# Order of the neighbour products in a residual block: one PSUM bank after the other, or both in turn

## Chip, core and metric

The kernel runs on one core of a Trainium2 chip. The metric is device time in microseconds (us) from the start to the end of one execution, lower is better; a figure for a kernel is the median of several executions.

## What is computed

The program is a chain of four layers on a batch of 4 sequences of 256 tokens with 512 features. The first two layers (a mixture of low-rank updates, and a cross-attention with 32 heads and a layer norm) give `x`. The last two are the same function, applied one after the other, and this is where the change lies:

```
idx = _knn_indices(xyz, 8)            # 8 nearest of 512 points, the same in both layers
for i in range(4):
    shortcut = points                  # [4, 256, 512]: 256 channels, 512 points
    p = _lrelu(points)
    g = _group_point(p, idx_t)         # the 8 neighbours of each point
    c  = einsum('oi,bin->bon',   w_center[i],   p)
    gn = einsum('oi,bikn->bokn', w_neighbor[i], g)
    points = (c + gn.sum(axis=2)) / 9 + shortcut
```

`w_center` and `w_neighbor` are the same array here (256 x 256 for each `i`). So a block is `points += W (p (I + N)) / 9`, where `N` is the 512 x 512 matrix of zeros and ones that says which points are neighbours of which. Two layers of four blocks make 8 blocks in a row for each of the 4 sequences.

## The kernel before

**Tiling.** `x1[b]` holds one sequence as two tiles of 128 channels x 512 points (`NL` = 2, the index `o` or `l`). `nbr[b, m]`, m = 0 to 3, holds the 128 rows 128m to 128m+127 of `I + N` as a 128 x 512 tile in fp32r (one pass of TensorE). `fT` holds the transposed weights.

**One block, `block(b, i)`.**
1. VectorE makes `p`, the leaky ReLU of both tiles of `x1[b]` (line 857).
2. TensorE makes `(W p)` transposed, in two halves of 256 points, `m2` = 0 and 1 (line 869): one PSUM bank `wp` holds two groups of 128 points x 256 output channels. Each half is 4 fp32 products, which the trace shows as 8 matmuls.
3. The half is split in two fp32r tiles, so that two one-pass products together keep fp32's accuracy: ScalarE casts it to `hi` (`wph`, line 882), VectorE subtracts `hi` from the PSUM bank to get `lo` (`wpl`, line 885).
4. The neighbour products (line 900, the function `gather`): for each output tile `o` a PSUM bank `pb[o]` (named `blk`) takes the sum over the four `m` and over `hi` and `lo` of `part.T @ nbr[b, m]`: 8 matmuls of 128 x 128 weights and 512 moving columns for each `o`, half of them from `m2` = 0 and half from `m2` = 1. `hi` and `lo` are the weights that are loaded, `nbr` is what streams.
5. VectorE adds a ninth of each bank to `x1[b]` (line 912). After the last block each tile goes out by a DMA of the SP queue (line 922).

**Order.** Nothing runs in the order of the source. `plan.add` records each step with an engine, an estimated cost, and what it reads and writes (the short forms `pe`, `act`, `dve`, `pool`); `Plan.emit` then plays a list scheduler: at each turn it takes, of the steps that could start first, the one of lowest rank (a due time from `DEADLINES` less the length of the chain behind it), and issues its instructions. One `pe(...)` is one unit that other PE work cannot be placed into. A PSUM bank is taken from the 8 by the first step that names it and given back after the last. So the four sequences run interleaved: while the half tile of one is split, PE works for another. Because `gather` is added once for each (`m2`, `o`), each such step is 4 matmuls into one bank, and `pb[0]` and `pb[1]` are separate outputs of separate steps.

Of the kernel before, what the change touches and what calls it, by code (L numbers as in the profile page):

```python
# [24 lines left out]
NL = S // 128  # L25
# [139 lines left out]
def xattn_seq_kernel(ctx: ExitStack, tc: tile.TileContext, a: dict, out: bass.AP):  # L165
# [23 lines left out]
    def make(kind, place, name):  # L189
# [4 lines left out]
    pe, act, dve, pool = (  # L194
        lambda *args, _e=e, **kw: plan.add(_e, *args, **kw) for e in ("PE", "ACT", "DVE", "POOL")
    )
# [11 lines left out]
    nbr = {}  # L208
# [642 lines left out]
    def block(b, i):  # L851
        pt, wi = x1[b], fT[:, i % NBLK]
        p = Buf("full", f"p{b}_{i}")
        for l in range(NL):
            dve(
                0.69,
                lambda l=l: V_.scalar_tensor_tensor(p.tile[:, l], pt[:, l], SLOPE, pt[:, l], ALU.mult, ALU.max),  # L857
                (("x", b, l), p),
                (("p", b, l),),
                port=True,  # L860
            )
        parts = []
        for m2 in range(2):
            ps = Buf("bank", f"wp{b}_{i}_{m2}")
            hi, lo = Buf("wp", f"wph{b}_{i}_{m2}"), Buf("wp", f"wpl{b}_{i}_{m2}")
            pe(
                1.73,
                lambda ps=ps, m2=m2: [
                    T_.matmul(  # L869
                        ps.tile[:, bass.ts(k, S)],  # L870
                        lhsT=p.tile[:, c, bass.ts(2 * m2 + k, 128)],
                        rhs=wi[:, c, :],
                        start=(c == 0),
                        stop=(c == NL - 1),
                    )
                    for k in range(2)
                    for c in range(NL)
                ],
                (("p", b, 0), ("p", b, 1), p, "fT"),
                (ps, hi, lo),  # L880
            )
            act(0.59, lambda ps=ps, hi=hi: A_.copy(hi.tile, ps.tile), (ps,), (hi,))  # L882
            dve(
                0.69,
                lambda ps=ps, hi=hi, lo=lo: V_.tensor_tensor(  # L885
                    lo.tile, ps.tile, hi.tile.bitcast(F32), ALU.subtract
                ),
                (ps, hi),
                (lo,),
            )  # L890
            parts.append((hi, lo))
        pb = [Buf("bank", f"blk{b}_{i}_{o}") for o in range(NL)]

        for m2 in range(2):
            for o in range(NL):

                def gather(m2=m2, o=o):
                    for m in (2 * m2, 2 * m2 + 1):
                        for k, part in enumerate(parts[m2]):
                            T_.matmul(  # L900
                                pb[o].tile,
                                lhsT=part.tile[:, bass.ds(m % 2 * S + o * 128, 128)],
                                rhs=nbr[b, m],
                                start=(m == 0 and k == 0),
                                stop=(m == H // 128 - 1 and k == 1),
                            )

                pe(0.92, gather, (*parts[m2], ("nbr", b, 2 * m2), ("nbr", b, 2 * m2 + 1)), (pb[o],))
        for o in range(NL):
            dve(  # L910
                0.69,
                lambda o=o: V_.scalar_tensor_tensor(  # L912
                    pt[:, o], pb[o].tile, 1.0 / (KNN + 1.0), pt[:, o], ALU.mult, ALU.add
                ),
                (pb[o],),
                (("x", b, o),),
            )
            if i == 2 * NBLK - 1:
                plan.add(
                    "SP",  # L920
                    0.45,
                    lambda o=o: S_.dma_start(out=out[b, bass.ts(o, 128), :], in_=pt[:, o, :]),
                    (("x", b, o),),
                )
# [4 lines left out]
    for b in range(B):  # L929
        plan.batch = b  # L930
        if b == B - 1:
            load_xT(b)
            load_x(b)
        mixture(b)
        values(b)
        queries(b)
        nearest(b)
        for i in range(2 * NBLK):
            plan.unit = (b, i)
            block(b, i)  # L940
        plan.unit = None
# [50 lines left out]
```

## Time and profile before

| | |
|---|---|
| time, median of 3 runs (lowest to highest) | 406.25 us (405.9 to 406.34) |
| the profiled execution's own time | 406.27 us |
| its span, first to last instruction | 404.5 us |
| granted TensorE clock, mean | 0.998 |
| PE busy | 398.3 us (98%), 2324 matmuls |
| VectorE busy | 264.7 us (65%) |
| ScalarE busy | 130.4 us (32%) |
| GpSimd busy | 93.0 us (23%) |
| neighbour products (line 900) | 512 matmuls |
| `wp` products (line 869) | 512 matmuls |

The span is what the trace covers; 1.8 us lie around it. The busy times are of one execution. The ends of matmul rows are modelled, so that a row's own length (0.39 to 0.58 us for line 900) is longer than the step from one start to the next; the steps between starts are what the work costs.

### The profile page before, as it was taken

How to read it: one execution, taken by the hardware profiler on the slowest of the kernel's cores; microseconds unless marked ns; L12 is line 12 of the kernel's file. 1: busy time of each engine (PE TensorE's matmuls, PEld its weight loads, DVE VectorE, ACT ScalarE, POOL GpSimd, SP SyncE). 2: the span in 40 equal slices, each digit the busy share in tenths (PEclk: the TensorE clock that was granted, in tenths of full speed). 3: DMA queues.
4: the chain of work that ended last, by engine and by line, in shares of the span. 5: the costliest groups of instructions: out<-in, count | busy, mean ns of one | idle time of the engine just before them, and what ended most of it. 6: DMA issues, size and time to landing. Idle time of an engine off the chain costs nothing.

```text
span 404.5 us, 5757 instructions
## 1 busy us (share of the span) xinstructions
PE 398.3 (98%) x2324; PEld 306.6 (76%) x2324; DVE 264.7 (65%) x476; ACT 130.4 (32%) x234; POOL 93.0 (23%) x94
## 2 busy tenths in 40 slices
PE   8999999999999999999999999999999999999996
PEld 6755786656857767866778888888888888888884
DVE  3855659997999999745588644646455463635433
ACT  4652153555464485131244222111111111111110
POOL 4644320727945808605000000000000000000000
PEclk9999999999999999999999999999999999999999
DMA  6995100000000000000000000000000000010102
GB/s 229 364 421 210 52 2 0 2 2 0 2 2 0 2 2 1 2 2 0 0 0 2 0 2 0 0 2 0 2 0 1 2 0 0 2 52 1 53 0 104
DMA packets 4746, 15.33 MB, mean 38 GB/s; under 512 B 688, under 2 KB 816, under 8 KB 4080
## 3 DMA queue, kind: packets, MB, share of 16 engines
q1 hardware_dynamic: 4720, 14.97, 9.9%
q8 instruction: 18, 0.29, 0.3%
q14 instruction: 8, 0.07, 0.1%
HBM read 12.87 MB, written 2.10 MB: 37 GB/s over the span
## 4 chain that ended last, share of the span: by engine, by line
PE 98%; DVE 1%; ACT 0%; issue 0%
PE blk L900 29%; PE wp L869 27%; PE upd L448 7%; PE o L818 7%; PE q L670 7%; PE pT L786 3%; PE d L512 3%; PE avT L798 2%; PE v L632 2%; PE route L392 2%; PE s L711 2%; PE kT L578 2%; PE d L525 1%; PE zT L438 1%; PE nbrT L556 1%; PE x1T L477 1%
## 5 line engine op out<-in xcount | busy, mean ns | idle before, releaser
L869 PE MATMUL wp<-fT,p 128*128 128x256 f32 x512 | 119.0, 380 | 0.0
L900 PE MATMUL blk<-nbr,wph 128*128 128x512 f32 x256 | 109.8, 429 | 0.0
L869 PEld LDWEIGHTS wp<-fT,p 128*128 128x128 f32 x512 | 96.6, 189 | 16.8 <-issue 1.2
L900 PE MATMUL blk<-nbr,wpl 128*128 128x512 f32 x256 | 100.6, 393 | 0.9 <-DVE wpl L885 0.9
L912 DVE SCALAR_TENSOR_TENSOR x<-blk,x 128x512 f32<-128x512 f32 x64 | 43.8, 687 | 76.9 <-PE blk L900 76.9
L882 ACT CAST wph<-wp 128x512 fp32r<-128x512 f32 x64 | 37.6, 587 | 168.4 <-PE wp L869 168.4
L885 DVE TENSOR_TENSOR wpl<-wp,wph 128x512 fp32r<-128x512 f32 x64 | 44.0, 687 | 24.5 <-ACT wph L882 24.5
L900 PEld LDWEIGHTS blk<-nbr,wpl 128*128 128x128 f32 x256 | 48.2, 188 | 11.4 <-DVE wpl L885 1.6
L900 PEld LDWEIGHTS blk<-nbr,wph 128*128 128x128 f32 x256 | 48.2, 188 | 11.3 <-ACT wph L882 0.8
L857 DVE SCALAR_TENSOR_TENSOR p<-x 128x512 f32<-128x512 f32 x64 | 44.8, 732 | 0.4
L774 POOL TENSOR_TENSOR s<-s,rden 128x512 f32<-128x512 f32 x32 | 35.1, 1132 | 36.4 <-DVE rden L764 35.6
L818 PE MATMUL o<-WoT,avTs 128*128 128x512 f32 x64 | 29.6, 597 | 0.0
L448 PE MATMUL upd<-lora_BT,zTs 128*128 128x512 f32 x64 | 29.2, 600 | 0.0
L670 PE MATMUL q<-x1T,WqT 128*128 128x256 f32 x128 | 28.7, 380 | 0.0
L670 PEld LDWEIGHTS q<-x1T,WqT 128*128 128x128 f32 x128 | 23.9, 190 | 3.5 <-issue 0.5
L737 DVE TENSOR_REDUCE mx<-s 128x8 f32<-128x512 f32 x32 | 19.9, 684 | 4.9 <-PE s L711 4.8
L448 PEld LDWEIGHTS upd<-lora_BT,zTs 128*128 128x128 f32 x64 | 11.6, 190 | 12.5 <-issue 11.8
L743 DVE TENSOR_TENSOR s<-s,mx 128x512 f32<-128x512 f32 x32 | 20.1, 684 | 0.0
L752 DVE TENSOR_REDUCE den<-s 128x8 f32<-128x512 f32 x32 | 19.9, 679 | 0.2
L818 PEld LDWEIGHTS o<-WoT,avTs 128*128 128x128 f32 x64 | 11.4, 190 | 10.6 <-issue 10.4
L749 ACT ACTIVATE s<-s 128x512 f32<-128x512 f32 x32 | 18.8, 633 | 1.8 <-DVE s L743 1.6
L791 ACT COPY pTs<-pT 128x512 f32<-128x512 f32 x32 | 17.0, 597 | 7.1 <-PE pT L786 7.1
(97 smaller groups left out, 376.7 us busy)
## 6 DMA issues: line engine op xcount, KB each, us to landing
xT<-in_xT SPq DMA_DIRECT2D x4, 512.0 KB, 6.7
x<-in_x SPq DMA_DIRECT2D x4, 512.0 KB, 12.2
out<-x SPq DMA_DIRECT2D x8, 256.0 KB, 2.0
WkT<-in_WkT SPq DMA_DIRECT2D x4, 256.0 KB, 7.7
lora_BT<-in_lora_BT SPq DMA_DIRECT2D x1, 1024.0 KB, 7.9
WqT<-in_WqT SPq DMA_DIRECT2D x1, 1024.0 KB, 9.9
WvT<-in_WvT SPq DMA_DIRECT2D x1, 1024.0 KB, 11.0
rows<-in_rows SPq DMA_DIRECT2D x2, 512.0 KB, 12.0
```

Source lines behind the costliest of these rows:

```text
L448: T_.matmul(ps2.tile, lhsT=zT.tile[:, bass.ts(c, 128)], rhs=w["lora_BT"][:, c, :], start=(c == 0), stop=(c == NC - 1),)
L670: T_.matmul(ps.tile[:, 0:S], lhsT=w["WqT"][:, c, bass.ts(o, 128)], rhs=x1T[b].tile[:, c, :], start=(c == 0), stop=(c == NC - 1),)
L737: lambda mx=mx, ps=ps: V_.tensor_reduce(mx.tile[:, 0:HPC], heads(ps), AX.X, ALU.max),
L743: lambda mx=mx, ps=ps, s=s: V_.tensor_tensor(heads(s), heads(ps), mx.tile[:, 0:HPC].unsqueeze(2).to_broadcast([128, HPC, V]), ALU.subtract),
L774: lambda s=s, g=g: G_.tensor_tensor(heads(s), heads(s), rden.tile[:, bass.ts(g, HPC)].unsqueeze(2).to_broadcast([128, HPC, V]), ALU.mult,),
L818: T_.matmul(po.tile, lhsT=avT.tile[:, bass.ts(c, 128)], rhs=w["WoT"][:, c, :], start=(c == 0), stop=(c == NC - 1),)
L857: lambda l=l: V_.scalar_tensor_tensor(p.tile[:, l], pt[:, l], SLOPE, pt[:, l], ALU.mult, ALU.max),
L869: T_.matmul(ps.tile[:, bass.ts(k, S)], lhsT=p.tile[:, c, bass.ts(2 * m2 + k, 128)], rhs=wi[:, c, :], start=(c == 0), stop=(c == NL - 1),)
L882: act(0.59, lambda ps=ps, hi=hi: A_.copy(hi.tile, ps.tile), (ps,), (hi,))
L885: lambda ps=ps, hi=hi, lo=lo: V_.tensor_tensor(lo.tile, ps.tile, hi.tile.bitcast(F32), ALU.subtract),
L900: T_.matmul(pb[o].tile, lhsT=part.tile[:, bass.ds(m % 2 * S + o * 128, 128)], rhs=nbr[b, m], start=(m == 0 and k == 0), stop=(m == H // 12 ...
L912: lambda o=o: V_.scalar_tensor_tensor(pt[:, o], pb[o].tile, 1.0 / (KNN + 1.0), pt[:, o], ALU.mult, ALU.add),
```

## The change

The loop over `o` moves from outside the planned step to the innermost place inside it. A step is now one `m2` with both banks: 8 matmuls that go to `pb[0]` and `pb[1]` in turn, instead of two steps of 4 matmuls into one bank each. The planned cost is 1.84 instead of twice 0.92, and the step names both banks as its outputs. Each matmul and its weights stay as they were; their number, 8 for each `m2`, too. In a bank the order of the additions is the same.

```diff
         for m2 in range(2):
-            for o in range(NL):
-
-                def gather(m2=m2, o=o):
-                    for m in (2 * m2, 2 * m2 + 1):
-                        for k, part in enumerate(parts[m2]):
+
+            def gather(m2=m2):
+                for m in (2 * m2, 2 * m2 + 1):
+                    for k, part in enumerate(parts[m2]):
+                        for o in range(NL):
                             T_.matmul(
                                 pb[o].tile,
                                 lhsT=part.tile[:, bass.ds(m % 2 * S + o * 128, 128)],
                                 rhs=nbr[b, m],
                                 start=(m == 0 and k == 0),
                                 stop=(m == H // 128 - 1 and k == 1),
                             )
 
-                pe(0.92, gather, (*parts[m2], ("nbr", b, 2 * m2), ("nbr", b, 2 * m2 + 1)), (pb[o],))
+            pe(1.84, gather, (*parts[m2], ("nbr", b, 2 * m2), ("nbr", b, 2 * m2 + 1)), pb)
```

## Prediction

> **What bounds the kernel now.** I read the page first: busy times, then the chain of waits, then the groups of the lines that the change touches.
>
> ```profile
> PE 398.3 (98%) x2324; PEld 306.6 (76%) x2324; DVE 264.7 (65%) x476; ACT 130.4 (32%) x234; POOL 93.0 (23%) x94
> ...
> L900 PE MATMUL blk<-nbr,wph 128*128 128x512 f32 x256 | 109.8, 429 | 0.0
> ...
> L900 PE MATMUL blk<-nbr,wpl 128*128 128x512 f32 x256 | 100.6, 393 | 0.9 <-DVE wpl L885 0.9
> ...
> L912 DVE SCALAR_TENSOR_TENSOR x<-blk,x 128x512 f32<-128x512 f32 x64 | 43.8, 687 | 76.9 <-PE blk L900 76.9
> ```
>
> TensorE is the bound: it is busy for 398.3 of 404.5 us and the page's chain of the work that ended last is 98% PE. Line 900 is its largest part, and in front of it PE waits only 0.9 us, for `lo`. VectorE waits 76.9 us for these products, so it has room. Two ways to gain are then open: cheaper steps between the 512 matmuls of line 900, or fewer PE waits (few are left). Any loss must be a new PE wait, or work behind the last matmul.
>
> Next, whether a step into the same bank costs more than one into another. The timeline of PE's last 16 neighbour products shows both, since the bank changes after every fourth (its second to ninth row; the first column is the start in us):
>
> ```profile
> 396.99 0.39 PE L900 MATMUL blk<-nbr,wpl 128*128 128x512 f32 x1
> 397.21 0.40 PE L900 MATMUL blk<-nbr,wph 128*128 128x512 f32 x1
> 397.45 0.39 PE L900 MATMUL blk<-nbr,wpl 128*128 128x512 f32 x1
> 397.68 0.40 PE L900 MATMUL blk<-nbr,wph 128*128 128x512 f32 x1
> 397.92 0.39 PE L900 MATMUL blk<-nbr,wpl 128*128 128x512 f32 x1
> 398.15 0.40 PE L900 MATMUL blk<-nbr,wph 128*128 128x512 f32 x1
> 398.39 0.39 PE L900 MATMUL blk<-nbr,wpl 128*128 128x512 f32 x1
> 398.62 0.40 PE L900 MATMUL blk<-nbr,wph 128*128 128x512 f32 x1
> ```
>
> The first of the 16 is left out, because its row starts early, over the end of a `wp` product. From 396.99 on, the steps from `hi` to `lo`, always in one bank, are 0.24, 0.24 and 0.24. Those from `lo` to `hi` are 0.22 (397.21) and 0.23 (398.15) in the same bank, and 0.23 (397.68) and 0.23 (398.62) where the bank changes. A change of bank saves nothing. The last matmul of the 16 starts at 400.25, so 14 steps take 3.26 us: 0.233 each.
>
> Then what waits for the banks. VectorE in one round of the steady part, where line 900 and line 869 alternate:
>
> ```profile
> 387.14 0.69 DVE L912 SCALAR_TENSOR_TENSOR x<-blk,x 128x512 f32<-128x512 f32 x1 [3.19 <-PE blk L900]
> 387.75 0.68 DVE L885 TENSOR_TENSOR wpl<-wp,wph 128x512 fp32r<-128x512 f32 x1
> 388.35 0.68 DVE L912 SCALAR_TENSOR_TENSOR x<-blk,x 128x512 f32<-128x512 f32 x1
> 388.94 1.28 DVE L857 SCALAR_TENSOR_TENSOR p<-x 128x512 f32<-128x512 f32 x2
> ```
>
> The new `p` is ready at 390.22; the `wp` products that read it start at 391.46 in the timeline: 1.24 us of margin. Last, the end and the dense stretch:
>
> ```profile
> 399.75 0.69 DVE L912 SCALAR_TENSOR_TENSOR x<-blk,x 128x512 f32<-128x512 f32 x1 [1.48 <-PE blk L900]
> 400.69 0.69 DVE L912 SCALAR_TENSOR_TENSOR x<-blk,x 128x512 f32<-128x512 f32 x1 [0.25 <-PE blk L900]
> ...
> 134.00:140.00 6.00, 5.10 (x24) 3.62 (x23) 5.50 (x8) 2.99 (x4) 5.64 (x6) 1.00 0.01 3
> 140.00:163.00 23.00, 23.00 (x219) 16.45 (x218) 22.03 (x40) 15.29 (x29) 10.09 (x9) 1.00 0.00 1
> ```
>
> In the last two rows (busy time of PE, weight loads, DVE, ACT, POOL by stretch) VectorE is busy for 5.50 of 6 us and then 22.03 of 23 us, while the first sequences are already in their blocks. Both PE waits for `lo` lie in the first of them.
>
> **The change part by part.** No instruction is added or dropped; 512 matmuls and weight loads stay. Three things move.
>
> (1) *The steps of line 900.* Before, a bank takes 4 in a row: `hi`, `lo`, `hi`, `lo`. After, it is `hi`, `hi`, `lo`, `lo` with the banks in turn. A rule that would promise a gain stands in the Trainium skill, "TensorE: Matmul & The Clock Gate", section "Wait — 56ns, not 53.3ns?": warm matmuls follow each other after N / 2.4 GHz plus about 2.5 ns, 215.7 ns at 512 columns. The rows say 233. By the rule, were the excess due to the bank, the change would give 512 x 17 ns = 8.9 us. But the excess is there where the bank changes too, so I take the row: no gain from banks. What is left is that 0.22 to 0.24 depends on something the trace doesn't name. Around 202 us the timeline has `hi` and `lo` steps alike: from 201.35 to 203.62 ten steps, 0.227 each. The order of the weight loads, which the change alters, may move the mean between these: 512 x (0.227 - 0.233) = -3.1 us and 512 x (0.238 - 0.233) = +2.6 us. Over the steady groups, with several patterns of long and short steps, the means that I worked out from the starts all lie between 0.231 and 0.232 over seven steps, so I take 0.
>
> (2) *What is behind a gather.* Before, the first bank of a block is complete 0.93 us ahead of the second (line 912 starts at 399.75 and 400.69). After, it is complete one step ahead, 0.23 us. The skill speaks against the change here: "Perfetto Trace Analysis", section "Optimizing Tensor Performance" (Matmuls), wants independent groups to rotate through banks so that emptying one overlaps the next group's matmuls. Both line 912 of a block now come after nearly all its products. By that rule alone each of 32 blocks would have its second addition later by one addition less one step, 0.69 - 0.23 = 0.46 us: 14.7 us. The trace says what covers it: between two blocks of one sequence PE works for another. In the round shown, the first addition moves from 387.14 to about 387.84 (three steps), `lo` at 387.75 moves ahead of it into the 3.19 us that VectorE was idle, and the two additions and the two `p`, at about 0.6 us each, end near 390.3 instead of 390.22. The margin of 1.24 us becomes about 1.15. Cost 0 there, with 1 us to spare; the cover is missing only after the last gather. There the last addition, now at 400.69, must wait for the other one: this starts 0.43 us (399.75 less 399.32, the start of its last matmul) after a matmul that moves to about 400.02, so at 400.45, and ends at 401.14. The last addition thus starts 0.4 to 0.45 us later, and the output DMA behind it too: **+0.43**. The two output DMAs on SP now come 0.69 instead of 0.94 us apart; an issue takes SP 0.33 us, so the second isn't held up by the first.
>
> (3) *The waits and the plan.* In each gather the first `lo` product is now the third, not the second, so `lo` may be 0.23 us later. PE's two waits for it (0.53 and 0.37 us in the timeline) each shrink by 0.23: at best -0.46. VectorE is nearly full in this stretch, so part is likely to come back as a later wait; I take **-0.3** (0 to -0.46). The scheduler has coarser PE steps and needs both banks at once. The order of the changed program is the same on PE, apart from the turns of the banks, until the output of batch 2's attention, differs through the stretch where blocks of batches 0 and 1 mix with the attention and neighbour search of batches 2 and 3, and from the fourth or so of the eight blocks on alternates `wp` and gather as before. In the stretch of 140 to 260 us PE had no idle time at all (23.00 of 23 in the last row above, and 97.00 of 97 in the next, from 163 to 260). A different order can only keep that or lose some: a gather placed right behind its own `wp` pair has some 1.5 us from matmul to `lo` (0.59 cast, 0.69 subtraction, two signals) against the 1.73 us of the next `wp`. One or two misses of 0.3 us are likely to be all: **+0.1**, bounds -0.2 (fewer switches between kinds of matmul, which cost about 0.1 each) and +1.0.
>
> Sum: 0 + 0.43 - 0.3 + 0.1 = +0.2 us. The profiled execution took 406.27 us, the median is 406.25, so they stand level: 406.5 us.
>
> **The rivals.**
> - *Same-bank additions do stall* and every bank change that I read was late for another reason. For: 17 ns of unexplained step. Against: the two bank changes above. 406.5 - 8.9 = 397.6 us.
> - *The step gets shorter by its loads*: two loads in a row now come from one tile. All at 0.227 as around 202 us: 406.5 - 3.1 = 403.4; half of it, 405.0.
> - *The step gets longer, the slower side*: in the rows, the long step is the one in which the streaming `nbr` stays (0.24 for `hi` to `lo`; 0.22 to 0.23 where it changes). If that repeat is what makes it long, three of four steps are long after, two of four before: 0.238 for a quarter of 512 steps in place of 0.229 is 128 x 9 ns = +1.2 us, 407.7 us; all at 0.238, 409.1. It decides from 7 ns on such a step (128 x 7 = 0.9). Against it: around 202 us the same repeats show no long steps.
> - *The reordered middle costs waits*: at its bound +1.0, 407.4 us. For: VectorE at 22.03 of 23. Against: from 163 us on it has a third free.
>
> **How the numbers follow.** A measurement of this kernel can tell about 0.2%, 0.8 us, from no change: 405.4 to 407.1 is "same". The forecast with small misses: 0.52, of which 0.48 lies within. Bank stall 0.04, shorter step 0.13 (two thirds below 405.4), longer step 0.18 (nearly all above 407.1), middle 0.13 (two thirds above). That makes faster 0.15, same 0.52, slower 0.33. The range from 404.6 to 408.0 leaves out the bank stall, the far half of the shorter and the longest of the longer step. The likeliest case by itself spans 405.6 to 407.0.
>
> **What would show it.** Right: line 900's starts still 0.22 to 0.24 apart on average 0.233, whether or not the moving tile repeats; PE's wait for `lo` near 0.45 instead of 0.9 us; PE full from 163 to 400 us; the last two line 912 rows back to back and the second 0.4 us later behind the last matmul. Wrong: an average step off by over 3 ns (rivals one to three, by its sign and size), or PE waits for `p`, `lo` or a bank over 0.5 us between 140 and 260 us.

## The result: 1.4 us slower

| | before | after |
|---|---|---|
| time, median of 7 runs each (lowest to highest) | 406.34 us (405.9 to 407.01) | 407.79 us (407.6 to 408.29) |
| profiled execution, its span | 404.5 us | 406.2 us |

The ratio is 1.0037, 95% interval 1.0025 to 1.0048: slower by 1.0 to 2.0 us. The forecast was 406.5, with 404.6 to 408.0 as its range; the result lies in it, on the side that had 0.33.

The page of the changed kernel, the rows that answer to those of before:

```profile
PE 399.1 (98%) x2324; PEld 306.3 (75%) x2324; DVE 267.0 (66%) x476; ACT 129.9 (32%) x234; POOL 92.4 (23%) x94
...
L900 PE MATMUL blk<-nbr,wph 128*128 128x512 f32 x256 | 90.8, 435 | 0.5 <-DVE wpl L885 0.5
L900 PE MATMUL blk<-nbr,wpl 128*128 128x512 f32 x256 | 80.4, 395 | 0.2 <-DVE wpl L885 0.2
...
L912 DVE SCALAR_TENSOR_TENSOR x<-blk,x 128x512 f32<-128x512 f32 x64 | 41.2, 686 | 22.3 <-PE blk L900 22.3
```

The busy time of the two line 900 groups is now 171.2 instead of 210.4 us. That is no gain. A row is longer than the step to the next one, and a group's busy time counts overlapping rows of the group once. Before, `hi` and `lo` rows alternated and hardly overlapped within a group; now two of each kind follow each other, and their overlap is counted once. The steps between starts tell what the work costs. The timeline of PE's last 16 products after the change, which now merges rows in pairs of the same kind:

```profile
398.45 0.63 PE L900 MATMUL blk<-nbr,wpl 128*128 128x512 f32 x2
398.92 0.63 PE L900 MATMUL blk<-nbr,wph 128*128 128x512 f32 x2
...
400.79 0.63 PE L900 MATMUL blk<-nbr,wph 128*128 128x512 f32 x2
401.25 0.63 PE L900 MATMUL blk<-nbr,wpl 128*128 128x512 f32 x2
```

From the first row to the last of these lie six pairs, so a pair takes (401.25 - 398.45) / 6 = 0.467 us, 0.233 a step: the number of before. Over all steps between neighbours of line 900 that hold no wait, the mean is 232.1 ns before and 232.2 after, and both range from 224 to 241. The long and the short ones keep their places in a group, although the weights and the bank at each place are now others. From 266 us on, every half tile of `wp` starts exactly 1.24 us later than before, to the last one. So the loss came about ahead of that and behind the last matmul. The waits of PE name most of the first part (total us, number of waits, the longest):

```profile
PE blk L900 <- DVE wpl L885: 0.7, 2, 0.5
PE wp L869 <- DVE p L857: 0.6, 1, 0.6
```

The second line is new; the first was 0.9 us before. The two additions at the end are the second part, now one behind the other:

```profile
401.69 1.29 DVE L912 SCALAR_TENSOR_TENSOR x<-blk,x 128x512 f32<-128x512 f32 x2 [2.18 <-PE blk L900]
```

To compare kernels I split each trace at the starts of the first and of the last product of line 900, since what lies ahead of the first is the same program in both and took between 134.4 and 135.7 us in the profiled executions of this document:

| kernel | first product | last product | between | from there to the end of the span |
|---|---|---|---|---|
| before | 134.66 | 400.25 | 265.59 | 4.26 |
| after | 134.95 | 401.49 | 266.54 | 4.72 |

The middle costs 0.95 and the end 0.46 us: together 1.41, close to the 1.45 us between the medians.

### The profile page after: what moved, and what is told of

Same layout as the page of the kernel before. It is cut to its first block, busy times and chain, and to the rows that moved or that the text cites. A ratio compares the mean times of both kernels' runs of the same rounds, so it can differ in the third digit from the quotient of the medians.

```text
span 406.2 us, 5760 instructions
## 1 busy us (share of the span) xinstructions
PE 399.1 (98%) x2324; PEld 306.3 (75%) x2324; DVE 267.0 (66%) x476; ACT 129.9 (32%) x234; POOL 92.4 (23%) x94
## 4 chain that ended last, share of the span: by engine, by line
PE 96%; DVE 2%; ACT 1%; DMA 1%; DVEq 0%; issue 0%; ACTq 0%
PE blk L900 29%; PE wp L869 27%; PE upd L448 7%; PE q L670 7%; PE o L818 6%; PE pT L786 3%; PE d L512 3%; PE avT L798 2%; PE v L632 2%; PE route L392 2%; PE s L711 2%; PE kT L578 2%; PE d L525 1%; PE zT L438 1%; PE x1T L477 1%; PE nbrT L556 1%
## 5 line engine op out<-in xcount | busy, mean ns | idle before, releaser
L869 PE MATMUL wp<-fT,p 128*128 128x256 f32 x512 | 120.3, 380 | 0.6 <-DVE p L857 0.6
L900 PE MATMUL blk<-nbr,wph 128*128 128x512 f32 x256 | 90.8, 435 | 0.5 <-DVE wpl L885 0.5
L900 PE MATMUL blk<-nbr,wpl 128*128 128x512 f32 x256 | 80.4, 395 | 0.2 <-DVE wpl L885 0.2
L912 DVE SCALAR_TENSOR_TENSOR x<-blk,x 128x512 f32<-128x512 f32 x64 | 41.2, 686 | 22.3 <-PE blk L900 22.3
L857 DVE SCALAR_TENSOR_TENSOR p<-x 128x512 f32<-128x512 f32 x64 | 46.6, 766 | 3.1 <-POOL x L844 3.1
```

The source lines that it names most:

```text
L869: T_.matmul(ps.tile[:, bass.ts(k, S)], lhsT=p.tile[:, c, bass.ts(2 * m2 + k, 128)], rhs=wi[:, c, :], start=(c == 0), stop=(c == NL - 1),)
L900: T_.matmul(pb[o].tile, lhsT=part.tile[:, bass.ds(m % 2 * S + o * 128, 128)], rhs=nbr[b, m], start=(m == 0 and k == 0), stop=(m == H // 12 ...
L912: lambda o=o: V_.scalar_tensor_tensor(pt[:, o], pb[o].tile, 1.0 / (KNN + 1.0), pt[:, o], ALU.mult, ALU.add),
```

## Where the new wait comes from

Around 158 us PE waits for `p` of block 0 of sequence 1. The timeline of all engines in the changed kernel shows the chain behind it:

```profile
154.98 0.59 ACT L791 COPY pTs<-pT 128x512 f32<-128x512 f32 x1 [3.51 <-PE pT L786]
...
155.59 1.28 ACT L834 ACT_TABLE_LOAD   x1
...
156.88 0.29 ACT L834 ACTIVATE mv<-mv,eps 128x1 f32<-128x1 f32 x1
...
157.21 0.17 DVE L835 RECIPROCAL mv<-mv 128x1 f32<-128x1 f32 x1 [2.28 <-ACT mv L834]
...
157.42 2.13 DVE L857 SCALAR_TENSOR_TENSOR p<-x 128x512 f32<-128x512 f32 x2
...
159.61 3.29 PE L869 MATMUL wp<-fT,p 128*128 128x256 f32 x14 [0.65 <-DVE p L857]
```

In the new order ScalarE has a copy in front of the square root of a layer norm of sequence 2. The copy waits 3.51 us for PE's transposes; after it comes the load of the table that the square root needs, 1.28 us. VectorE's next instruction is the reciprocal of that root, so VectorE stands still for 2.28 us, and both leaky ReLUs (`p`), which need nothing of it, stand behind. They end at 159.55, and PE's third `wp` matmul has waited 0.65 us. By the starts it is 0.81 us: the step from the second to the third is 1.02 instead of 0.22. The step behind it is longer too, 0.32 us, as it is behind both waits for `lo` (0.34 instead of 0.23); so the wait costs 0.91 in all.

Before, the same root was ahead of the copy, its table had been loaded at 151.30 in an idle stretch of ScalarE, and one of the two leaky ReLUs had been done at 149.55:

```profile
149.55 0.63 DVE L857 SCALAR_TENSOR_TENSOR p<-x 128x512 f32<-128x512 f32 x1
...
151.30 1.28 ACT L834 ACT_TABLE_LOAD   x1
...
155.37 0.30 ACT L834 ACTIVATE mv<-mv,eps 128x1 f32<-128x1 f32 x1 [2.78 <-DVE mv L833]
...
156.62 0.15 DVE L835 RECIPROCAL mv<-mv 128x1 f32<-128x1 f32 x1
```

The waits for `lo` shrank less than the forecast. In the first gather the second product, now also a `hi`, waits:

```profile
135.22 0.68 DVE L885 TENSOR_TENSOR wpl<-wp,wph 128x512 fp32r<-128x512 f32 x1
...
135.96 0.50 PE L900 MATMUL blk<-nbr,wph 128*128 128x512 f32 x1 [0.54 <-DVE wpl L885]
```

It needs no `lo`. But both banks are now taken at once, and in the plan `pb[1]` is the bank in which `wp` of this half lay; the subtraction that makes `lo` is its last reader. So the product waits for the bank just as long (0.54 us; before 0.53 for `lo`). Only the other wait, in the second gather, went from 0.37 to 0.17 us. The sum of the middle is thus -0.21 for `lo`, +0.91 for `p` and 0.25 more. As far as the starts show, this last part is spread over places where the new order puts other kinds of matmul side by side, with steps that are longer by 0.1 us at most. The profile lists no wait there, and no run parts it.

## Experiments

The change does two things: it makes the planned step coarser (eight products that take both banks), and it alternates the banks within. The first two kernels do one each.

**Alternate under the old plan.** The plan keeps its two steps; the products of both are issued at one of them.

```diff
                 def gather(m2=m2, o=o):
+                    if m2 == 0 and o == 0 or m2 == 1 and o == 1:
+                        return
                     for m in (2 * m2, 2 * m2 + 1):
                         for k, part in enumerate(parts[m2]):
-                            T_.matmul(
-                                pb[o].tile,
-                                lhsT=part.tile[:, bass.ds(m % 2 * S + o * 128, 128)],
+                            for q in range(NL):
+                                T_.matmul(
+                                    pb[q].tile,
+                                    lhsT=part.tile[:, bass.ds(m % 2 * S + q * 128, 128)],
...
```

> The plan of before, step for step and on every other engine in the same order, but the eight products of a half go to the two banks in turn (in the first half they are issued at the second of the two old steps, in the second half at the first). Theory (a turn of the banks is worth nothing; the 1.4 us came from the plan and the end): line 900's steps by position as before, 0.224 to 0.241 us, the last matmul at the same place as before within 0.3 us, and only the end later by 0.43 us: 406.8 us. Rival (alternating banks itself costs or gains on each step): the last matmul moves by more than 0.5 us, and the time by the 1.4 us seen with the change or more; a real gain from banks would show as up to 8.9 us less.

406.76 us against 406.12 of before, ratio 1.0013 (1.0006 to 1.0019), which is +0.5 us. From first to last product 265.50 us (before 265.59); from there to the end 4.73. The last additions are as in the change:

```profile
400.63 1.29 DVE L915 SCALAR_TENSOR_TENSOR x<-blk,x 128x512 f32<-128x512 f32 x2 [2.18 <-PE blk L903]
```

The mean step of line 900 is 232.1 ns, as before. So a turn of the banks changes nothing in 512 steps, neither way; what it costs is the end. (The second wait for `lo` is 0.21 us shorter, as in the change, and 0.13 of it is lost again in other steps.)

**Rows under the new plan.** One step of eight products, first those of one bank, then those of the other.

```diff
-                for m in (2 * m2, 2 * m2 + 1):
-                    for k, part in enumerate(parts[m2]):
-                        for o in range(NL):
+                for o in range(NL):
+                    for m in (2 * m2, 2 * m2 + 1):
+                        for k, part in enumerate(parts[m2]):
```

> The plan of the change (one step of eight products per half, both banks taken at once), but in a step the four products of one bank come first and then those of the other. Theory (plan and end): the plan's waits stay, so the last matmul is where the change has it, within 0.3 us (0.23 us later possible where lo is waited for); the end gets back 0.43 us because the first bank is complete 0.93 us ahead: 407.4 us. Rival (the turn of the banks costs on each step): with banks in rows the time falls back to that of before, 406.3 us.

407.52 us, ratio 1.0031 (1.0019 to 1.0042), +1.3 us. From first to last product 266.66 us, to the end 4.26. The end is that of before, and the wait for `p` is still there, without any alternation:

```profile
PE blk L900 <- DVE wpl L885: 0.9, 2, 0.5
PE wp L869 <- DVE p L857: 0.6, 1, 0.6
```

The rival's 406.3 lies outside the interval, the theory's 407.4 within. The loss of the middle is the plan's.

**The change with one reciprocal later.** The reciprocal that VectorE waited for is issued behind the two leaky ReLUs. The order on PE, ScalarE and GpSimd stays.

```diff
-        dve(0.16, lambda: V_.reciprocal(mv.tile[:, 3:4], mv.tile[:, 2:3]), (), (mv,))
+        def inverse():
+            V_.reciprocal(mv.tile[:, 3:4], mv.tile[:, 2:3])
+
+        dve(0.16, (lambda: late.append(inverse)) if (b, l) == (2, 0) else inverse, (), (mv,))
...
-                lambda l=l: V_.scalar_tensor_tensor(p.tile[:, l], pt[:, l], SLOPE, pt[:, l], ALU.mult, ALU.max),
+                lambda l=l: (
+                    V_.scalar_tensor_tensor(p.tile[:, l], pt[:, l], SLOPE, pt[:, l], ALU.mult, ALU.max),
+                    [late.pop()() for _ in range(len(late) if (b, i, l) == (1, 0, 1) else 0)],
+                ),
...
+    late = []
```

> The change, with one VectorE instruction issued later: the reciprocal of the layer norm of the first tile of sequence 2 comes behind the two leaky ReLUs of block 0 of sequence 1, and not ahead of them. Theory (that reciprocal waits 2.28 us for ScalarE's square root, holds the two behind it, and PE waits for them 0.65 us idle, 0.8 us by its starts): the wait of line 869 for p near 158 us goes, and the time falls by 0.6 to 0.9 us to about 407.0. Rival (PE's wait is only moved, because POOL or the later norm comes late in turn): PE waits elsewhere between 158 and 200 us for as long, and the time stays at 407.8.

406.72 us, ratio 1.0013 (1.0006 to 1.002): about 1 us under the change, by ratios and by medians. The forecast had 0.6 to 0.9; it left out the longer step behind the wait. The timeline: the ReLUs start at 156.17, and all 16 `wp` matmuls run through.

```profile
156.17 2.13 DVE L862 SCALAR_TENSOR_TENSOR p<-x 128x512 f32<-128x512 f32 x2
...
159.03 3.67 PE L876 MATMUL wp<-fT,p 128*128 128x256 f32 x16
```

From first to last product 265.63 us, 0.91 less than the change and within 0.04 of before. PE's list of waits holds no other in its place; the rival falls.

**Both losses taken out.** Rows within the step, and the reciprocal later: the two diffs above together.

> The plan of the change, with both losses that the runs so far named taken out: in a step the four products of one bank and then those of the other (the end), and the reciprocal of sequence 2 issued behind the two leaky ReLUs (the wait for p). Theory (the losses are these two and add up): from the first product of line 900 to the last 265.6 to 265.8 us as before and as with the reciprocal alone, the end 4.26 us behind it as before: level with before, ratio 1.000, within 0.3 us. Rival (a third part of the 1.4 us lies elsewhere in the plan): at least 0.5 us above before remains.

406.26 us against 406.10, ratio 1.0008 (0.9997 to 1.002): level with before within the interval, where 1.000 was expected. From first to last product 265.72 us (before 265.59), to the end 4.26; PE's list of waits has none for `p`, and those for `lo` are the 0.9 us of before. The plan of the change has no third loss of the size that the rival asks; about 0.1 us of the middle remains.

**What the 17 ns are: bf16 operands.** Before, with both halves of the split and the neighbour matrix in bf16.

```diff
-        "wp": (work, [128, 2 * S], F32R, 8),
+        "wp": (work, [128, 4 * S], BF16, 8),
...
-                nbr[b, k] = keep.tile([128, H], F32R, tag=nbr_tag[b][k], name=f"nbr{b}_{k}")
-                A_.copy(nbr[b, k], ps.tile)
+                nbr[b, k] = keep.tile([128, 2 * H], BF16, tag=nbr_tag[b][k], name=f"nbr{b}_{k}")
+                A_.copy(nbr[b, k][:, 0:H], ps.tile)
...
-            act(0.59, lambda ps=ps, hi=hi: A_.copy(hi.tile, ps.tile), (ps,), (hi,))
+            act(0.59, lambda ps=ps, hi=hi: A_.copy(hi.tile[:, 0 : 2 * S], ps.tile), (ps,), (hi,))
...
-                    lo.tile, ps.tile, hi.tile.bitcast(F32), ALU.subtract
+                    lo.tile[:, 0 : 2 * S], ps.tile, hi.tile[:, 0 : 2 * S], ALU.subtract
...
-                                rhs=nbr[b, m],
+                                rhs=nbr[b, m][:, 0:H],
```

> Before, with hi, lo and the neighbour matrix in bf16 instead of fp32r in line 900 ([...]the plan is unchanged). It asks what the 17 ns are by which a step of 0.233 us stands over 0.2157. Theory (the loading of fp32 weights, 188 ns a tile, sets the step; a bf16 load takes 98 ns in the rows of line 556): the step falls to 0.216, 512 x 0.017 = 8.7 us less, 397.6 us. Rival (the adding in PSUM, or the stream of 512 columns, sets it): the step stays at 0.233 and the time at 406.3.

398.41 us, ratio 0.9804 (0.979 to 0.9817), 8.0 us faster than before (7.7 by the medians). The steps are 0.216 us, with four products in a row into one bank as before (three of them, from the timeline):

```profile
391.18 0.38 PE L900 MATMUL blk<-nbr,wph 128*128 128x512 bf16 x1
391.40 0.38 PE L900 MATMUL blk<-nbr,wpl 128*128 128x512 bf16 x1
391.61 0.38 PE L900 MATMUL blk<-nbr,wph 128*128 128x512 bf16 x1
```

Over 458 steps the mean is 216.0 ns, as the 215.7 ns that the Trainium skill gives for 512 columns ("TensorE: Matmul & The Clock Gate", "Wait — 56ns, not 53.3ns?"); for fp32r operands, at 232, the rule is 16 ns short. Adding into one bank thus goes on at 0.216 us per 512 columns, and the bank is out as the reason for 0.233. From first to last product the run takes 257.20 us, 8.4 less than before where 8.7 was expected. That fits my theory of the load, but this run changes the stream as well as the weights. The next two kernels part them.

**Half the weights, half the stream.** Each leaves out part of the products of m = 1 and 2.

```diff
-                                pb[o].tile,
-                                lhsT=part.tile[:, bass.ds(m % 2 * S + o * 128, 128)],
+                                pb[o].tile if m in (0, 3) else pb[o].tile[0:64],
+                                lhsT=part.tile[:, bass.ds(m % 2 * S + o * 128, 128 if m in (0, 3) else 64)],
```

> Before, with 64 instead of 128 columns of weights in the products of m = 1 and 2 (channels 64 to 127 of each tile leave these two out); the stream stays 512 columns. Theory (the load of fp32r weights sets the step): a step into a half load takes 0.216 us, one into a full load 0.23. Rival (the stream of 512 fp32r columns sets it): 0.224 to 0.241 us for all steps.

```diff
-                                pb[o].tile,
+                                pb[o].tile if m in (0, 3) else pb[o].tile[:, 0:256],
...
-                                rhs=nbr[b, m],
+                                rhs=nbr[b, m] if m in (0, 3) else nbr[b, m][:, 0:256],
```

> Before, with 256 instead of 512 streaming columns in the products of m = 1 and 2 (the last 256 points leave these two out); the weights stay 128 x 128. Theory (the load sets the step): a step out of a half stream into a full load stays at 0.19 to 0.24 us, the time of a load and its hand-over. Rival (the stream sets it): 0.11 to 0.12 us.

Each was run once, for its steps: with half the weights 406.02 us (before 406.10), with half the stream 378.00. With half the weights the load is 0.13 instead of 0.19 us, and the steps stay (timeline; 128*64 are the half loads):

```profile
382.72 0.39 PE L900 MATMUL blk<-nbr,wph 128*64 128x512 f32 x1
382.95 0.39 PE L900 MATMUL blk<-nbr,wpl 128*64 128x512 f32 x1
383.18 0.39 PE L900 MATMUL blk<-nbr,wph 128*128 128x512 f32 x1
383.42 0.39 PE L900 MATMUL blk<-nbr,wpl 128*128 128x512 f32 x1
```

The mean step is 230.6 ns between two half loads and 232.7 between two full ones. With half the stream and full loads:

```profile
360.34 0.39 PE L900 MATMUL blk<-nbr,wpl 128*128 128x512 f32 x1
360.57 0.28 PE L900 MATMUL blk<-nbr,wph 128*128 128x256 f32 x1
360.68 0.28 PE L900 MATMUL blk<-nbr,wpl 128*128 128x256 f32 x1
360.80 0.39 PE L900 MATMUL blk<-nbr,wph 128*128 128x512 f32 x1
```

A step out of a half stream takes 0.11 to 0.12 us (mean 121 ns), one out of a full stream 0.23. My theory of the load falls, and the rival holds: the stream sets the step, or the columns added into PSUM, which halve with it. From 256 to 512 columns it grows by 232 - 121 = 111 ns. What in the stream of four-byte elements takes 0.233 us where bf16 takes 0.216 stays open; the two differ in weights and stream at once, and no run had one in each type.

## Why the prediction was right and where it was off

The result lies in the range, on its slower side. The likeliest case, 406.5 us, did not come. Its sum was 0 + 0.43 - 0.3 + 0.1; the traces give 0 + 0.46 - 0.2 + 1.15 = 1.41.

- *Step (1), no gain from the banks:* right, to 0.1 ns in the mean. The two bank changes in the rows of before were enough to tell, and both runs that part plan from order agree. Of the rivals on it, the stall of same-bank additions falls by the bf16 run too. The rival of the longer step (a repeated `nbr` makes it long) falls: three of four steps repeat it now, and the mean is the same. That its 407.7 us lies close to what was measured is chance. The rival of the shorter step falls by the same mean. Long and short steps keep their places in a group; why is open.
- *Step (2), the end, +0.43:* the size was right, 0.46, in part by luck. The second addition started 0.81 us behind the last matmul's start instead of 0.43, so 0.37 us later, because the two additions start 0.61 us apart and not 0.69. The other 0.09 came with the last DMA, which was not in the sum: it took 2.13 instead of 2.04 us to land. The time from the last product to the end is 4.72 to 4.73 in all three kernels that have the additions back to back, and 4.26 to 4.28 in those that have not. The cover in the steady rounds held: no wait in any of them. The Trainium skill's rule on rotating banks ("Perfetto Trace Analysis", "Optimizing Tensor Performance"), which by itself would have made 14.7 us, counted here only at the end, where no other sequence's work lay behind the last gather.
- *Step (3), the wait for `lo`, -0.3:* off by a little, -0.2. One of the two shrank. That the second bank is the one that the split is about to release was in the plan and I didn't look for it.
- *Step (3), the reordered plan, +0.1:* this is the term that was mis-sized. It measured about +1.15, a little over its bound of +1.0: 0.91 us went with one reciprocal, the rest is the 0.25 us that no run parts. I had named it as the fourth rival at 407.4 us, with VectorE at 22.03 of 23 us as the evidence for it, and a wait for `p` of over 0.5 us between 140 and 260 us as a sign of being wrong; that sign came (0.65 us). For the likely value I thought of gathers that start too close behind their own `wp`, and no wait of that kind came behind the first two gathers. What cost was the order on VectorE: a short instruction whose input is late, with unrelated work behind it.
- *The rival that came* is the reordered middle. Its 407.4 us holds the end already. The measured 1.4 us over before makes 407.7 of it, because the plan cost more than the bound and the waits for `lo` shrank less.
- *A slip in the chances:* from the cases as listed, "slower" adds up to about 0.28 and "same" to 0.57, not 0.33 and 0.52.

## What to carry to other kernels

Where a matmul group's neighbours in the trace already change the bank from time to time, the step across such a change tells what alternating banks would bring, before any code is written; here it was nothing. In a kernel that a list scheduler orders, a change to the size of one step is a change to the order of every engine: look in the new order of each engine for a short instruction with a late input that stands ahead of unrelated work, and for a buffer that the step takes while its last reader is the instruction that makes the step's input. A row's wait is then not its whole price: here the step behind the wait was 0.1 us longer too. What is completed together at the very end of the program is paid once, here with 0.46 us, however well the same work is covered elsewhere.

## Not expected

- The split in bf16 takes 8.0 us off (398.41 us, ratio 0.9804), more than any order of the products could, and is faster than both kernels. What it does to the accuracy of the result was not measured here.
- An fp32r product of 512 columns takes 0.233 us from start to start, a bf16 one 0.216. Halving the fp32r weights that are loaded takes nothing off it (231 ns); halving the stream leaves 121 ns. What makes the difference between fp32r and bf16 is open.
- The last two output DMAs of 256 KB, issued 0.60 instead of 0.94 us apart: the second lands 2.13 instead of 2.04 us after its issue.
